# Layer 2's centring pass: eight lines of half the channels a turn, 16 stores instead of 32, half of the last ones issued by ScalarE

## The chip, the cores and the metric

The kernel runs on one core of a Trainium2 chip. Its engines are TensorE (PE, matrix products), VectorE (DVE), ScalarE (ACT) and GpSimd (POOL); SyncE (SP) computes nothing and issues DMAs. Data moves between HBM and the core's memory (SBUF) through 16 DMA engines. The metric is the device time of one execution, in microseconds: 11168.38 us before the change, the median of three runs (11148.58 to 11170.93).

## The reference, cut to what matters

The input is x, 16 images of 64 x 64 positions with 256 channels, float32. Four layers are applied, each as `x = x + layer(groupnorm(x))` with 32 groups. Layer 0 is linear attention with a layer norm, layer 1 a gated block with a scan and two channel reductions, layers 2 and 3 are involutions: at each position a small matrix product makes the weights of a 3 x 3 (layer 2) or 7 x 7 (layer 3) window, one set for each of 16 groups of channels. Layer 3, the one that reads what this change writes, is

```
r    = relu(batchnorm(x @ w_reduce))
kgen = (r @ w_span + b_span).reshape(B, H, W, 16, 49)
xp   = pad(x, 3 rows and columns of zeros on every side)
out  = einsum('bhwgk,bhwkgc->bhwgc', kgen, 7x7 patches of xp)
```

with x here the group-normed input `(x - m) / sqrt(var)`. The subtraction of the mean m must precede the zero padding, since the pad is zero after the norm; the division by the deviation can be moved into the masks and weights.

## The kernel before, in words

The kernel goes through the layers in stages. Layer 0 takes up to about 3600 us of the profiled span, layer 1's scan to about 4190, then comes the stage that ends layer 1 and does layer 2 (to about 7947), then layer 3. Intermediate images lie in HBM: `x2_d` is layer 1's result, `x3_d` layer 2's result as positions by channels, `c3_d` the same as channels by positions, and `strips` the centred and padded copy that layer 3 reads. `strips` holds, for each image and each half of the channels, 73 rows by 14 columns by 8 column tiles by 128 channels: each tile of eight columns is stored with its three neighbours on either side, so that neighbouring tiles overlap.

The stage of layer 2 is a loop of 161 turns (L1154) whose order is written by hand. A turn works on four jobs, each for one eighth of an image, staggered by `LAG = (0, 12, 20, 33)` turns:

- the end of layer 1 (`end_of_layer1`, L897), turns 0 to 127: VectorE, ScalarE, GpSimd, and statistics on VectorE;
- the projection (`projected`, L948), turns 12 to 139;
- the involution, turns 20 to 147: TensorE makes the reduced tile (`reduced2`, L969, from the tile x2r) and the weights (L986) and transposes patches (L1002); VectorE multiplies (`products`, L1040) and sums (L1052, L1053); part of the sums is done by TensorE (L1057);
- the centring (`centred`, L1109), turns 33 to 160: GpSimd subtracts the group mean from a piece of `x3_d` (L1112), and DMAs store it into `strips`.

SyncE issues all DMAs, in the order of the program. In turn n it first issues the loads for the next turns (`loads(n + 1)`, recorded at L872: x2p, x2r, the two x1 pieces and the two pf pieces), then the stores collected in the turn before (L1160: x2_d, x3_d, c3_d and the centring's), then the load of the piece to be centred in the next turn (`load_centred`, tile xc, L890). The profile's names leave numbers out: x2_d and x3_d both read x_d, c3_d reads c_d. The tile xc has two buffers, so that its load in turn n waits until the stores of the buffer's last content, issued just ahead of it in the same turn, have landed. What still lies in the list after the last turn is stored at L1209.

A centring turn takes four lines out of each half of the image (g = 0, 1: lines 0 to 31 and 32 to 63), all 256 channels: 64 columns of each g lie on 128 partitions, a tile of 128 x 4 x 256. A store carries one g, one column tile and one half of the channels: 14 columns (11 at the edges) by 4 lines by 128 channels. That makes 2 x 8 x 2 = 32 stores a turn, in pieces of 512 bytes.

From turn 149 on only the centring is left. Then comes layer 3, whose first loads wait for this stage's memory.

Of the kernel before, what the change touches and what calls it, by code (L numbers as in the profile page):

```python
# [11 lines left out]
ALU = mybir.AluOpType  # L12
# [3 lines left out]
P = 128  # L16
C = 256
HW = 64
NT = HW * HW
NCH = 8  # L20
# [24 lines left out]
def network(ctx: ExitStack, tc: tile.TileContext, a: dict, out: bass.AP):  # L45
    nc = tc.nc
    NI = a["x"].shape[0]
# [44 lines left out]
    strips = dram.tile([NI, 2, HW + 9, TC + 6, NTC, P], F32, tag="strips", name="strips")  # L92
# [10 lines left out]
    def step():  # L103

        for c in list(chains):
            if next(c, c) is c:
                chains.remove(c)
# [47 lines left out]
    with ExitStack() as st:  # L155
# [12 lines left out]
        for v in (wo[:, 0], wo[:, 1], bout):  # L168
            mean = small.tile([P, 1], F32, tag="wmean", name="wmean")
# [17 lines left out]
        loaded, stores = {}, []  # L187

        def load(kind, i, ch):

            if kind == "xin":
                t = []
                for k in range(2):
                    t.append(wk.tile([P, 2, C], F32, tag="xin", name="xin", bufs=4))
                    t0 = ch * CT + k * 256
                    nc.sync.dma_start(
                        out=t[k], in_=a["x"][i, t0 : t0 + 256, :].rearrange("(d p) c -> p d c", p=P)
                    )
            else:
                tag = "xn" if kind == "xn" else "x1"  # L200
                t = wk.tile([P, 2, CT], F32, tag=tag, name=kind, bufs=2 if kind == "xn" else 4)
                src = x_d[i, ch]
                if kind == "xm":
                    src = x1_d[i, :, :, ch * CT : (ch + 1) * CT].rearrange("h p t -> p h t")
                nc.sync.dma_start(out=t, in_=src)
            loaded[kind, i, ch] = t
# [305 lines left out]
        def jobs(n):  # L512
            m, t = divmod(n, NCH)
            i, hf = divmod(m, 2)

            def at(k):
                return 0 <= k < NI

            todo = []
            if at(i):  # L520
                todo.append(("q", i, hf, t))
            if hf == 0:
                if at(i + 1):
                    todo.append(("xin", i + 1, t))
            elif at(i - 1):
                todo.append(("x1", i - 1, t))

            if at(i - 2) and (t >= 2 if hf == 0 else t < 2):
                todo.append(("xm", i - 2, (t - 2) % NCH))
            return todo  # L530
# [4 lines left out]
        def loads(n):  # L535
            for job in jobs(n):
                if job[0] == "q":
                    load("xn", job[1], job[3])
                else:
                    load(*job)  # L540
# [12 lines left out]
        for n in range(2 * NCH * (NI + 1) + NCH + 2):  # L553
            m, t = divmod(n, NCH)
# [54 lines left out]
    with ExitStack() as st:  # L609
# [23 lines left out]
        with tc.tile_pool(name="s_conv", bufs=1) as pcv:  # L633
# [4 lines left out]
                out=lsa.rearrange("p i j c -> p (i j c)"), in_=a["lsa_w"].partition_broadcast(P)  # L638
# [3 lines left out]
            for dj in range(7):  # L642
                dst = band if dj == 0 else term
# [22 lines left out]
        for n in range(10):  # L666
            delta, c = n // 2, n % 2
# [26 lines left out]
        for ch in range(NCH):  # L694
            for b in range(0, NI, 8):
                n = min(8, NI - b)
# [10 lines left out]
                for k, dst in enumerate((pa, pbc[:, 0, :], pbc[:, 1, :])):  # L707
                    nc.tensor.matmul(
                        dst, lhsT=w40[0 : 5 * n, k, :], rhs=rows[0 : 5 * n], start=True, stop=True
# [27 lines left out]
        for k in range(0, NI * NB, P):  # L737
            n = min(P, NI * NB - k)
# [89 lines left out]
    with ExitStack() as st:  # L828
# [7 lines left out]
        gmb = {}  # L836
# [29 lines left out]
        loaded, stores = [], []  # L866
# [8 lines left out]
        def taken(name):  # L875

            n = [k for k, _ in loaded].index(name)
            return loaded.pop(n)[1]
# [9 lines left out]
            ))  # L888

        def load_centred(i, rc):  # L890
            x3n = x3_d[i].rearrange("(g r w) c -> g w r c", g=2, w=HW)
            load("xc", [P, 4, C], *(
                (lambda t, g=g: t[g * HW : (g + 1) * HW], x3n[g][:, rc * 4 : rc * 4 + 4])
                for g in range(2)
            ))

        def end_of_layer1(i, rc):  # L897

            if rc == 0:
                st0[i] = wk.tile([P, 2, NCH, 6], F32, tag="st0", name="st0")  # L900
            x1, pf = taken("x1"), taken("pf")
            zs = [wk.tile([P, 2, 256], F32, tag="z", name="z", bufs=1), pf]
            for h, z in enumerate(zs):
                nc.vector.scalar_tensor_tensor(
                    z, x1[:, h], gm1[:, i, h : h + 1], pf, ALU.subtract, ALU.mult
                )
            yield
            x2 = wk.tile([P, 2, CT], F32, tag="x2", name="x2")
            for h, z in enumerate(zs):
                nc.scalar.activation(  # L910
                    z, z, AF.Relu, bias=bnp[:, 1, h : h + 1], scale=ab[:, 0, i, h : h + 1]
                )
                nc.gpsimd.tensor_tensor(
                    x2[:, h].rearrange("p (t g) -> p g t", g=2), z, x1[:, h], ALU.add
                )
            stores.append((x2_d[i, rc], x2))
            yield
            for h in range(2):
                nc.vector.bn_stats(st0[i][:, h, rc, :], x2[:, h])
            if rc == NCH - 1:  # L920
                chains.append(norm2(i))
                next(chains[-1])
# [185 lines left out]

        def centred(i, rc):  # L1109

            xc = taken("xc")
            nc.gpsimd.tensor_tensor(  # L1112
                xc, xc, gmb[i].unsqueeze(1).broadcast_to([P, 4, C]), ALU.subtract
            )
            for g in range(2):
                r0 = 3 + 32 * g + 4 * rc
                for tj in range(NTC):
                    lo, hi = max(0, tj * TC - 3), min(HW, tj * TC + TC + 3)
                    c0 = lo - tj * TC + 3
                    for h in range(2):  # L1120
                        stores.append((
                            strips[i, h, r0 : r0 + 4, c0 : c0 + hi - lo, tj, :].rearrange(
                                "r w c -> w r c"
                            ),
                            xc[g * HW + lo : g * HW + hi, :, h * P : (h + 1) * P],
                        ))

# [3 lines left out]
        LAG = (0, 12, 20, 33)  # L1133
# [17 lines left out]
        with tc.manual_schedule():  # L1151
            loads(0)
            ahead, made = None, None
            for n in range(TURNS):  # L1154
                end, proj, inv, cen = jobs(n)
                nxt = jobs(n + 1)[2]
                done, stores[:] = list(stores), []
                loads(n + 1)
                for dst, src in done:
                    nc.sync.dma_start(out=dst, in_=src)  # L1160
                nxt_cen = jobs(n + 1)[3]
                if nxt_cen:
                    load_centred(*nxt_cen)
                now, ahead = ahead, None
                ending = end_of_layer1(*end) if end else None
                if ending:
                    next(ending)
                if inv:
                    w1 = weights(now[1], 1)
                    x3 = wk.tile([P, 4, C], F32, tag="x3", name="x3", bufs=3)  # L1170

                def prepare():
                    x2r, rt = reduced2(*nxt)
                    ahead = [x2r, rt]
                    ahead.append(patches(*nxt, lambda: ahead.append(weights(rt, 0))))
                    return ahead

                if nxt and nxt[1]:
                    ahead = prepare()
                if ending:  # L1180
                    next(ending)
                if made:
                    nc.scalar.copy(made[2][:, 0:ON_PE, 0:P], made[3][:, 0:ON_PE])  # L1183
                if inv:
                    los = residual(now[0])
                c3 = turned(*made[:3]) if made else None
                step()
                if proj:
                    projected(*proj)
                if inv:  # L1190
                    pd = products(0, now[2], now[3])
                    sums_on_tensor(pd, los[0])
                if nxt and not nxt[1]:
                    ahead = prepare()
                if inv:
                    pd1 = products(1, w1, now[3])
                    sums(0, pd, los[0], x3)
                step()
                if made:
                    statistics3(*made[:2], c3)  # L1200
                if inv:
                    sums(1, pd1, los[1], x3)
                if ending:
                    next(ending, None)
                made = (*inv, x3, los[0]) if inv else None
                if cen:
                    centred(*cen)
            for dst, src in stores:
                nc.sync.dma_start(out=dst, in_=src)  # L1209
# [309 lines left out]
```

## Time and profile before

The profiled execution spans 11130.4 us. By stage (us; busy times of the engines, share of the DMA engines):

| stretch | length | PE | DVE | ACT | POOL | DMA |
|---|---|---|---|---|---|---|
| 0 to 3600, layer 0 | 3600.00 | 3122.58 | 2236.30 | 1900.12 | 409.75 | 0.41 |
| 3600 to 4190, layer 1's scan | 590.00 | 157.94 | 418.71 | 39.61 | 16.45 | 0.54 |
| 4190 to 7947, end of layer 1 and layer 2 | 3757.00 | 2618.05 | 3259.98 | 1293.71 | 642.96 | 0.53 |
| 7947 to 11130, layer 3 | 3183.40 | 2475.12 | 1610.90 | 1456.49 | 0.00 | 0.56 |

Busy times are sums over the stretch; an engine can be busy beside the others. The profile counts issuing a DMA as no work of an engine, so SyncE has no busy time here; its issues are seen in its timeline, where one line gives start, duration, line, tile and count, and in the chain of waits, where "SPq" is time in which the next step waited for SyncE to issue. The names "out<-in" give a DMA's destination and source.

The DMAs of the centring, with the duration of an issue on SyncE (smallest, median, largest, in ns): 4064 stores into strips at L1160 with 282/387/2124 and 32 at L1209 with 295/387/389; 256 loads of xc with 579/608/988. The subtraction on GpSimd takes 2350 ns (median, 128 times).

### The profile page before, as it was taken

What the parts mean: (1) busy time and instruction counts of PE and PEld (TensorE: products, weight loads), DVE (VectorE), ACT (ScalarE), POOL (GpSimd) and SP (SyncE); (2) the same over time, 40 slices, a digit from 0 to 9 for tenths busy, and PEclk for the clock granted to TensorE, in tenths of its full rate; (3) what the DMA queues carried; (4) which work ended last, traced back from release to release, by engine and by line L of the source; (5) the groups of instructions that cost most, each with busy time, mean ns of one, the idle gap of its engine ahead of it and who ended that gap; (6) DMA issues with size and microseconds to landing.
All of it is one profiled execution on the core that took longest, in us unless ns stands there. A gap on an engine that the chain in (4) does not pass through costs nothing.

```text
span 11130.4 us, 218459 instructions
## 1 busy us (share of the span) xinstructions
PE 8373.7 (75%) x88184; PEld 6128.7 (55%) x88184; DVE 7525.9 (68%) x11694; ACT 4689.9 (42%) x10571; POOL 1069.2 (10%) x681
## 2 busy tenths in 40 slices
PE   8888888888886506777777777774377777777777
PEld 5666666666665204555555555553266655566555
DVE  5566656666665497999999999996155545555444
ACT  4555555555554104343333333332144444444444
POOL 0111111111110002111111111111000000000000
PEclk9999999999998557888888888887699999989999
DMA  7334334433432285455555555544455565555555
GB/s 241 130 133 145 132 127 137 149 127 121 149 107 91 76 289 192 144 175 182 175 174 174 174 174 175 174 142 125 125 172 177 180 204 186 183 180 172 189 186 172
DMA packets 1353717, 1796.61 MB, mean 161 GB/s; under 512 B 132875, under 2 KB 1031812, under 8 KB 1351556
## 3 DMA queue, kind: packets, MB, share of 16 engines
q1 hardware_dynamic: 1352708, 1782.63, 49.8%
q8 instruction: 697, 11.42, 0.4%
q14 instruction: 312, 2.56, 0.1%
HBM read 1268.05 MB, written 536.87 MB: 162 GB/s over the span
## 4 chain that ended last, share of the span: by engine, by line
PE 32%; DVE 18%; DMA 15%; issue 13%; SPq 10%; ACT 9%; POOL 3%; DVEq 0%; ACTq 0%; POOLq 0%
SPq L1160 8%; PE pa L1353 6%; DVE wm L1309 6%; PE pq L267 5%; DMA c_d<-c 5%; PE pk L1294 4%; DMA x<-x_d 4%; PE py L423 4%; PE pr L1262 2%; ACT sq L432 2%; SPq L872 2%; ACT wm L1304 2%; PE px L955 2%; DMA strips<-xc 2%; DVE y L428 1%
## 5 line engine op out<-in xcount | busy, mean ns | idle before, releaser
L267 PE MATMUL pq<-wq,xn 128*128 128x384 f32 x4096 | 1478.0, 500 | 63.1 <-DVE diag L316 21.0
L1040 DVE TENSOR_TENSOR pd<-xs,pw 128x576 f32<-128x576 f32 (+15 forms) x3072 | 1438.0, 549 | 4.5 <-PE pw L986 2.8
L1309 DVE TENSOR_TENSOR wm<-pk,spanb 128x704 f32<-128x704 f32 x896 | 1148.8, 1343 | 216.4 <-PE pk L1294 216.4
L1294 PE MATMUL pk<-rt,span 64*128 64x176 f32 x12288 | 1172.3, 328 | 152.7 <-DVE wm L1309 58.3
L1353 PE MATMUL pa<-wm,xw 126*32 126x48 f32 x45056 | 812.6, 226 | 507.8 <-issue 404.9
L1294 PEld LDWEIGHTS pk<-rt,span 64*128 64x128 f32 x12288 | 934.6, 188 | 385.4 <-ACT wm L1304 183.8
L1304 ACT ACTIVATE wm<-pk,spanb 128x176 f32<-128x176 f32 x2560 | 976.2, 542 | 334.5 <-PE pk L1294 325.9
L1052 DVE TENSOR_REDUCE x<-pd 128x384 f32<-128x3456 f32 (+1 forms) x256 | 1110.9, 4339 | 0.0
L1353 PEld LDWEIGHTS pa<-wm,xw 126*32 126x32 f32 x45056 | 673.4, 123 | 741.8 <-issue 543.6
L1363 DVE SCALAR_TENSOR_TENSOR ex<-pa,msk,ex 128x192 f32<-128x192 f32 x704 | 287.6, 416 | 1171.2 <-ACT ex L1362 1168.8
L267 PEld LDWEIGHTS pq<-wq,xn 128*128 128x128 f32 x4096 | 753.0, 194 | 495.8 <-issue 55.2
L1362 ACT ACTIVATE ex<-pa,msk 128x192 f32<-128x192 f32 x704 | 290.6, 421 | 1034.4 <-PE pa L1353 1031.6
L1006 ACT COPY xs<-pt 128x512 f32<-128x512 f32 x1152 | 606.8, 589 | 117.5 <-PE pt L1002 115.5
L1002 PEld LDWEIGHTS pt<-ident,pad 128*128 128x128 f32 x4608 | 532.4, 149 | 215.3 <-issue 155.6
L1002 PE MATMUL pt<-ident,pad 128*128 128x128 f32 x4608 | 618.2, 289 | 19.1 <-ACT xs L1006 7.7
L976 PE MATMUL pr<-x2r,wrs 128*64 128x512 f32 x512 | 362.9, 849 | 324.0 <-DMA x2r<-x_d 324.0
L979 ACT ACTIVATE rt<-pr,b,sb 64x512 f32<-64x512 f32 x128 | 99.3, 776 | 1134.5 <-PE pr L976 1134.5
L1057 PE MATMUL lo<-pd,ident 128*128 128x128 f32 x2304 | 552.7, 409 | 3.7 <-DVE pd L1040 3.7
L955 PE MATMUL px<-x2p,wis 128*128 128x512 f32 x1024 | 520.8, 653 | 20.5 <-ACT pad L959 10.1
L1057 PEld LDWEIGHTS lo<-pd,ident 128*128 128x128 f32 x2304 | 474.9, 207 | 107.7 <-issue 54.8
L423 PE MATMUL py<-wo,oT 128*128 128x256 f32 x2048 | 484.9, 388 | 61.5 <-DVE va L283 45.3
L1030 PE MATMUL lo<-ident,x2r 128*128 128x128 f32 x896 | 181.7, 330 | 464.0 <-ACT x L1183 294.6
(229 smaller groups left out, 13591.7 us busy)
## 6 DMA issues: line engine op xcount, KB each, us to landing
xw<-strips SPq DMA_DIRECT2D x704, 512.0 KB
xn<-x_d SPq DMA_DIRECT2D x256, 512.0 KB
x<-x_d SPq DMA_DIRECT2D x256, 512.0 KB
x_d<-x SPq DMA_DIRECT2D x256, 512.0 KB
strips<-xc SPq DMA_DIRECT2D x3072, 28.0 KB
xin<-in_x SPq DMA_DIRECT2D x256, 256.0 KB
x_d<-xc SPq DMA_DIRECT2D x128, 512.0 KB
xm<-x_d SPq DMA_DIRECT2D x128, 512.0 KB
```

Of the source, the lines that this page charges most:

```text
L267: nc.tensor.matmul(pq[:, dd, 0:384], lhsT=xn[:, h, tok], rhs=wq[:, h, hf * 384 : (hf + 1) * 384], start=(h == 0), stop=(h == 1),)
L423: nc.tensor.matmul(py[:, q, :], lhsT=oT[hf][:, q * P : (q + 1) * P], rhs=wo[:, hf, :], start=(hf == 0), stop=(hf == 1),)
L955: nc.tensor.matmul(px, lhsT=w[:, h, fh * P : (fh + 1) * P], rhs=x2[:, h], start=(h == 0), stop=(h == 1),)
L1002: nc.tensor.transpose(pt[:, k, h * P : (h + 1) * P], lines[:, h, rc * 4 + e + k, 2 * j : 2 * j + P], ident,)
L1040: nc.vector.tensor_tensor(pd[:, :, o - oh * P : o - oh * P + n, :], xs[dj][:, di : di + 4, c0 : c0 + 9 * n].rearrange("p r (f k) -> p r f ...
L1052: nc.vector.tensor_reduce(half, pd[:, n:], AX.X, ALU.add)
L1057: nc.tensor.matmul(lo[:, 0:ON_PE], lhsT=ident, rhs=pd[:, 0:ON_PE, :, k], start=False, stop=(k == 8))
L1160: nc.sync.dma_start(out=dst, in_=src)
L1294: nc.tensor.matmul(pkv[:, b, m], lhsT=span[half, h * 8 + q * 2 + gg, s0 : s0 + P], rhs=rto[half, o, :], start=True, stop=True,)
L1304: nc.scalar.activation(dst[:, m // 2, m % 2], pkv[:, m // 2, m % 2], AF.Identity, bias=spanb[:, g0 + m : g0 + m + 1],)
L1309: nc.vector.tensor_tensor(dst, pkv, spanb[:, g0 : g0 + 4].rearrange("p (b m) -> p b m", b=2).unsqueeze(3).broadcast_to([P, 2, 2, NTL]), AL ...
L1353: nc.tensor.matmul(pav[32 * q : 32 * q + 32, :, tj * TC : (tj + 1) * TC], lhsT=xws[k][0:TILE_IN, tj, 32 * q : 32 * q + 32], rhs=wm[q][0:TI ...
```

## The change

A centring turn now takes eight lines of one half of the channels instead of four lines of all channels. The turn number rc is split into `q, h = divmod(rc, 2)`: q picks the eight lines, h the half. The tile is 128 x 8 x 128, of the same size, and an image still takes eight turns. A store covers one g and one column tile with 8 lines, so there are 2 x 8 = 16 of them a turn, each of twice the bytes, still in pieces of 512 bytes. The load of xc is still two DMAs; its pieces in HBM are now 512 bytes where they were 1 KB. The second part: in the turns after 148, every other store in the list is issued by ScalarE instead of SyncE. The aim is fewer issues on SyncE, and two issuing engines where only the centring is left.

```diff
         def load_centred(i, rc):
+            q, h = divmod(rc, 2)
             x3n = x3_d[i].rearrange("(g r w) c -> g w r c", g=2, w=HW)
-            load("xc", [P, 4, C], *(
-                (lambda t, g=g: t[g * HW : (g + 1) * HW], x3n[g][:, rc * 4 : rc * 4 + 4])
+            load("xc", [P, 8, P], *(
+                (
+                    lambda t, g=g: t[g * HW : (g + 1) * HW],
+                    x3n[g][:, q * 8 : q * 8 + 8, h * P : (h + 1) * P],
+                )
                 for g in range(2)
             ))
...
+            q, h = divmod(rc, 2)
             xc = taken("xc")
+            mean = gmb[i][:, h * P : (h + 1) * P]
             nc.gpsimd.tensor_tensor(
-                xc, xc, gmb[i].unsqueeze(1).broadcast_to([P, 4, C]), ALU.subtract
+                xc, xc, mean.unsqueeze(1).broadcast_to([P, 8, P]), ALU.subtract
             )
             for g in range(2):
-                r0 = 3 + 32 * g + 4 * rc
+                r0 = 3 + 32 * g + 8 * q
                 for tj in range(NTC):
                     lo, hi = max(0, tj * TC - 3), min(HW, tj * TC + TC + 3)
                     c0 = lo - tj * TC + 3
-                    for h in range(2):
-                        stores.append((
-                            strips[i, h, r0 : r0 + 4, c0 : c0 + hi - lo, tj, :].rearrange(
-                                "r w c -> w r c"
-                            ),
-                            xc[g * HW + lo : g * HW + hi, :, h * P : (h + 1) * P],
-                        ))
+                    stores.append((
+                        strips[i, h, r0 : r0 + 8, c0 : c0 + hi - lo, tj, :].rearrange(
+                            "r w c -> w r c"
+                        ),
+                        xc[g * HW + lo : g * HW + hi],
+                    ))
...
-                for dst, src in done:
-                    nc.sync.dma_start(out=dst, in_=src)
+                for k, (dst, src) in enumerate(done):
+                    tail = n > LAG[2] + NI * NCH and k % 2
+                    (nc.scalar if tail else nc.sync).dma_start(out=dst, in_=src)
```

`LAG[2] + NI * NCH` is 20 + 128 = 148.

## The prediction

> **What bounds the kernel now.** I read the kernel by stage, not by its shares: layer 0 ends near 3600 us, layer 1's scan near 4190, layer 2 near 7947, layer 3 fills the rest. The edit touches only layer 2. There I cut the time at the first instruction of every eighth turn, so that each stretch is one image's eight involution turns, and asked for the busy times. Columns: stretch and length, PE, PEld, DVE, ACT, POOL with counts, clock, DMA share, GB/s.
>
> ```profile
> 4702.30:4907.10 204.80, 157.96 (x815) 118.70 (x816) 199.89 (x293) 81.43 (x163) 40.23 (x26) 0.89 0.57 180
> 5996.20:6221.20 225.00, 166.73 (x815) 121.39 (x815) 204.13 (x298) 80.99 (x163) 41.79 (x27) 0.84 0.56 174
> 7309.80:7508.90 199.10, 156.93 (x799) 112.90 (x800) 181.23 (x255) 69.29 (x146) 19.47 (x9) 0.86 0.48 139
> 7752.80:7946.70 193.90, 0.00 (x0) 0.00 (x0) 0.42 (x1) 0.00 (x0) 25.74 (x11) 0.50 0.32 84
> ```
>
> Read the DVE column against the length. The third image (4702) runs with VectorE 97.6% busy, with centring already in every turn. The ninth (5996) takes 20 us longer for the same work: VectorE is down to 91%. In the last image but one (7309) layer 1's work is gone, VectorE has less to do, and still it idles 9%. In the fourth row no compute engine but GpSimd does anything, and the DMA engines are busy a third of the time. What holds the later images and the end?
>
> The chain of the third image leads through VectorE's products. In the later images and at the end it leads through SyncE (SPq). In the order of the lines: third image, tenth (6221), image 7309, and the end.
>
> ```profile
> by line: DVE pd L1040 18.4%; DVE x L1052 14.8%; SPq L1160 9.8%; DMA c_d<-c 7.9%; DMA x<-x_d 7.2%; PE px L955 5.0%; issue 4.9%; PE lo L1057 4.1%; DMA pf<-fac_d 3.1%; DVE st L919 3.1%; DVE st L1087 2.3%; PE pt L1067 2.1%; DVE z L904 1.9%; DVE
> by line: DMA x<-x_d 18.8%; SPq L1160 17.7%; DMA c_d<-c 9.9%; PE px L955 7.6%; DMA strips<-xc 5.7%; PE lo L1057 5.6%; SPq L872 5.1%; issue 5.0%; ACT xs L1006 3.8%; PE pt L1002 3.4%; PE pr L976 3.4%; DMA x2r<-x_d 3.3%; PE pt L1067 1.9%; PE pw
> by line: SPq L1160 36.8%; DMA c_d<-c 24.2%; PE px L955 7.6%; DMA strips<-xc 6.1%; SPq L872 5.4%; issue 4.7%; DVE x L1052 4.3%; PE lo L1057 4.2%; PE pt L1067 2.0%; PE lo L1030 1.5%; PE pr L976 0.9%; DVE x L1053 0.9%; DVE st L1087 0.6%; ACT x
> by line: SPq L1160 54.8%; DMA xc<-x_d 17.9%; DMA strips<-xc 9.3%; issue 8.5%; SPq L1209 6.0%; SPq L872 4.2%
> ```
>
> SyncE's own timeline shows one of those turns, and then a turn of the end (start, duration, line, what, count):
>
> ```profile
> 6018.78 1.27 SPq L872 DMA_DIRECT2D xc<-x_d  x2
> 6020.09 0.61 SPq L872 DMA_DIRECT2D x2p<-x_d  x1
> 6020.74 0.43 SPq L872 DMA_DIRECT2D x2r<-x_d  x1
> 6021.28 0.93 SPq L872 DMA_DIRECT2D x<-x_d  x2
> 6022.26 2.07 SPq L872 DMA_DIRECT2D pf<-fac_d  x2
> 6024.37 2.33 SPq L1160 DMA_DIRECT2D x_d<-x  x3
> 6027.64 1.43 SPq L1160 DMA_DIRECT2D c_d<-c  x2
> 6029.17 16.76 SPq L1160 DMA_DIRECT2D strips<-xc  x32
> 6047.20 1.27 SPq L872 DMA_DIRECT2D xc<-x_d  x2
> ...
> 7754.15 13.70 SPq L1160 DMA_DIRECT2D strips<-xc  x32
> 7769.20 1.24 SPq L872 DMA_DIRECT2D xc<-x_d  x2
> ```
>
> From one xc load to the next is 28.4 us with hardly a hole: 16.8 us are the 32 stores, then 1.3 us until the stores have landed (the xc load refills their buffer). SyncE's issuing takes the whole turn, so **SyncE is the bound** of the later images; it falls behind slowly, which is why the third image doesn't show it yet. How its lateness reaches VectorE, in the waits of the tenth image (total, times, longest):
>
> ```profile
> PE pr L976 <- DMA x2r<-x_d: 23.8, 6, 6.4
> DVE x L1053 <- PE lo L1057: 13.1, 5, 4.3
> ```
>
> The x2r load is issued late, TensorE starts the next turn's weights late, reaches its sums (L1057) late, and VectorE waits for them. In the third image the first of these waits is absent. The end is plainer: twelve turns of 16.4 us, of which 13.7 are 32 issues, 0.43 us each, with everything else idle.
>
> **What the Trainium skill says.** "DMA: Bandwidth & Descriptors", section "Issuing engines are not separate DMA queues": a second issuing engine saves only issue time, "usually small relative to the DMA itself". The trace disagrees on small: at the end issuing is 13.7 of 16.4 us with the DMA engines at 0.32. Same page, "Rules for kernel authors": under 64 KB a transfer is mostly overhead. The stores are 22 and 28 KB and become twice that; the trace agrees. Same page, "Specifications": below 512 B a piece loses the line rate. The new xc load's pieces are exactly 512 B; the trace's packet records give 27 ns (median) for 512 B against 46 ns for 1 KB, so no cliff, but a piece costs a little more per byte.
>
> **The change part by part.**
>
> *Issue time of a store.* The new store has 8 rows of 512 B on 14 or 11 partitions where the old has 4. No issue of that shape is in the trace, but issue time does not go with bytes: stores on 14 partitions have a median of 387 ns; a load of 64 partitions of 1 KB x 4 (xc) 608 ns, yet one of 64 partitions with 4 bytes each (the constants v) 595 ns, and 128 partitions x 3 pieces of 512 B (ot) 371 ns. So I take 0.43 us a store with its gap; the bound from above is 0.65 (the dearest kind, 0.608 plus gap). Sixteen then take 6.9 us (10.4 at worst) instead of 13.7.
>
> *DMA engines.* Bytes and store packets stay. The load has 1024 packets of 27 ns instead of 512 of 46: 27.6 against 23.6 engine-us, over 16 engines +0.25 us a turn, at a share of 0.56: hidden.
>
> *GpSimd.* Still 1024 elements a partition, one instruction, 2.35 us as now; it waits for xc loads and is busy under 20%: nothing.
>
> *The wait before the xc load* stays: SyncE still waits for the stores just issued, and behind it in the queue stand the next turn's x2p, x2r, x1 and pf loads, on which TensorE and VectorE depend. Stores issued twice as fast land later after the last issue. Lower bound 1.4 us (now); upper 7 us, the time that the c_d stores take to land in the chain of this stage. I take 3. SyncE's turn becomes 27.4 (2191 us over the 80 turns below) - 6.9 + 1.6 = about 22 us, under VectorE's 25.4 (203 us of an image over 8). **The bound goes back to VectorE.**
>
> *Main loop.* The ten images from 5118.8 to 7309.8 take 2191.0 us and have 2023.8 us of VectorE work. At the 97.5% of the third image they take 2076: **-115 us**. Image 7309: 181.2 / 0.965 = 188 instead of 199: **-11**. Earlier images: nothing.
>
> *End.* In turns after 148 half of the stores go to ScalarE, which has no work there, so what queues behind its waits costs nothing. A turn is then 1.3 (xc load) + 8 x 0.43 = 3.4 (both engines at once) + landing. ScalarE's issue price is nowhere in the trace; between 0.4 and 0.65 us, 3.4 to 5.2. Landing: the busiest DMA engines take 16 stores x 8 packets plus 64 of the load, 192 x 29 ns (mean) = 5.6 us, part of it under the issue. So 6.1 us at least (landing 1.4), 11.7 at most (landing 7); I take 7.5. GpSimd is not in the way: xc landed 3.4 us after its issue, plus 2.35, is ready after a turn of this length. Twelve turns: 90 us; the last stores (now 13.4 us, all from SyncE still) 6.9 + 1.4 landing. Together 99 against 209.8 (7736.9 to 7946.7): **-111 us**. Turn 148 itself: **-7**.
>
> Sum: -115 - 11 - 111 - 7 = -244; 11168 - 244 = **10924, rounded to 10925 us**.
>
> **The rivals.**
>
> *Only the end gains.* If the late x2r load comes from the DMA queues (the chain has 10 to 24% on c_d landing) and not from SyncE's issue, the images keep their length: -118, **11050 us**. For it: c_d takes 6 to 7 us to land, and SyncE pauses inside its stores (16.8 instead of 13.7 us). Against it: in the third image the DMA share was as high (0.57) and VectorE did not wait.
>
> *More than that.* VectorE without holes and an end turn of 6.1 us: images -167 and -18, end -128, -7: -320, **10850 us**. For it: nothing else is near its limit. Against: even the image before all centring (4295 to 4494) had VectorE at 96%.
>
> *A wait replaces it, slower.* If the doubled stores, with 512 B loads in front of them, land 10 us after the last issue, SyncE's turn is 1.7 us longer (-6.9 + 8.6), over 95 turns +160; an end turn is 1.3 + 3.4 + 10 = 14.7, -20, and -13 for the single-engine stores: +127, **11295 us**. Against: the DMA engines need 5.6 us for a turn's data even alone.
>
> **How the numbers follow.** Forecast 0.68, only the end 0.12, more 0.14, slower 0.06. The range goes to both neighbours, since landing time (1.4 to 7 us) and ScalarE's price move the sum by some 50 us each way: 10850 to 11055. Faster by over 0.2%: 0.92; same 0.02 (for partial forms of the last rival); slower 0.06.
>
> **What would show it.** Right: 16 issues of 0.39 us a turn; TensorE's wait for x2r nearly gone; images of 205 to 211 us from the fifth on, VectorE at 97%; an end of about 100 us with both engines issuing. Wrong: issue time that grows with the rows; SyncE standing longer before the xc load, with x2r still late; end turns over 10 us. Layers 0, 1 and 3 should not move; if they do, my reading of what the edit touches was wrong.

## The result, and the profile after

The changed kernel takes **10912.13 us** (median of four runs, 10903.33 to 10919.3) against 11162.76 of the kernel before on the same chip (four runs, 11148.58 to 11170.93): a ratio of **0.9776**, 95% interval 0.9759 to 0.9793, or 250.6 us less. 10925 had been predicted.

In the profiled executions, the 3651.1 us from the first involution turn to layer 3's first load (4295.6 to 7946.7) became 3406.3 (4301.1 to 7707.4), 244.8 us less. Ahead of that the two profiles differ by 5.5 us. Layer 3 took 3183.7 us before and 3210.1 after, so the whole spans differ by 212.9 us only (11130.4 and 10917.5). The edit isn't the cause: in the profiles of the eleven kernels below layer 3 lies anywhere from about 3185 to 3211 whether or not they have the edit, and at 3185.5 when the changed kernel was profiled again. What moves it is not known. The single profiles are therefore compared stage by stage, and the whole by the medians.

Stretches of the changed kernel cut at the same turns as in the prediction (length, PE, PEld, DVE, ACT, POOL, clock, DMA share, GB/s). They are the ninth image, the last but one, and the end from turn 149 to layer 3. The last line sums the ten images from the fifth on.

```profile
5950.40:6154.70 204.30, 161.07 (x815) 121.31 (x816) 200.01 (x294) 81.08 (x162) 40.12 (x26) 0.87 0.62 189
7182.60:7361.80 179.20, 151.58 (x799) 114.80 (x800) 175.16 (x250) 68.67 (x147) 19.54 (x9) 0.91 0.55 158
7581.40:7707.40 126.00, 1.19 (x2) 0.50 (x2) 0.97 (x4) 0.00 (x0) 28.72 (x13) 0.50 0.55 138
...
sum 2061.60, PE 1623.75 PEld 1218.25 DVE 2008.52 ACT 805.82 POOL 393.66; mean PE 162.37 PEld 121.83 DVE 200.85 ACT 80.58 POOL 39.37
```

The third image has its 204.8 us as before. The ninth, 225.0 us before, is as short as the third again, with VectorE 97.9% busy, and so it goes on: from the fifth image to the thirteenth the lengths repeat as 208.3, 204.3 and 208.6 us, and the fourteenth, in which layer 1's work runs out, takes 198.0. Layer 2 no longer falls behind. The DMA share has gone up only because the same traffic passes in less time.

SyncE's timeline of one turn of the ninth image (start, duration, line, what, count):

```profile
6014.07 1.29 SPq L872 DMA_DIRECT2D xc<-x_d  x2
6020.77 0.35 SPq L872 DMA_DIRECT2D x2p<-x_d  x1
...
6026.11 2.02 SPq L1168 DMA_DIRECT2D c_d<-c  x2
6031.02 8.25 SPq L1168 DMA_DIRECT2D strips<-xc  x16
6040.92 1.29 SPq L872 DMA_DIRECT2D xc<-x_d  x2
```

Sixteen stores take 8.25 us with their pauses, where 32 took 16.76, and holes have opened: 5.4 us ahead of the x2p load and 2.9 us ahead of the strips stores. What stands in the holes is in SyncE's waits. From 5100 to 7300 us the longest are, first in the kernel before and then in the changed one (total, times, longest):

```profile
SPq L872 <- DMA strips<-xc: 89.8, 151, 2.5
SPq L1160 <- DMA x_d<-x: 89.6, 196, 1.0
SPq L1160 <- DMA c_d<-c: 62.5, 158, 1.2
SPq L1160 <- DMA x2r<-x_d: 55.7, 79, 1.4
```

```profile
SPq L872 <- PE px L959: 503.4, 86, 10.5
SPq L872 <- DMA strips<-xc: 132.2, 194, 2.8
```

Before, stores at L1160 waited in part for the landing of loads whose data they don't use, such as x2r; the reason is found below, with the end turn. SyncE now waits for TensorE (px is its projection, which reads x2p) to finish with the x2p buffer, some 5.9 us in each of the 85 turns of that stretch: it runs ahead of the engines that compute. And TensorE? Over the whole stage from 4200 us the first two of these lines were among its waits before, the third is after (lo are its partial sums). No wait for x2r appears any more. Its waits for ScalarE's copy ahead of the same sums are left out here, since both kernels have them alike (294.6 and 309.8 us).

```profile
PE pr L976 <- DMA x2r<-x_d: 324.0, 76, 8.0
...
PE lo L1030 <- DVE x L1053: 169.0, 33, 10.5
```

```profile
PE lo L1034 <- DVE x L1057: 314.6, 93, 10.5
```

TensorE waited for data; now it waits for VectorE to give buffers back. This is how a bound that moved looks: the same engine idles, for another reason. VectorE's own wait for TensorE's sums fell over the stage from 161.0 us to 56.0:

```profile
DVE x L1053 <- PE lo L1057: 161.0, 66, 6.3
```

```profile
DVE x L1057 <- PE lo L1061: 56.0, 24, 4.2
```

The chain of waits alone would not have told. The third image has the same length and the same share of VectorE in both kernels; its chain led through VectorE's products before, and in the changed kernel it reads

```profile
by line: PE px L959 13.4%; SPq L1168 10.7%; DMA c_d<-c 8.9%; DMA strips<-xc 8.5%; DVE pd L1044 8.0%; SPq L872 7.2%; DVE x L1056 6.5%; issue 5.8%; DMA pf<-fac_d 4.9%; PE pt L1071 4.8%; PE lo L1034 3.4%; DVE st L923 3.1%; POOL xc L1119 2.3%; 
```

So a chain's largest piece is a hint, and the share of VectorE and the runs with less of its work, below, decide.

The end is shorter but not as short as it was predicted. Its timeline in the changed kernel, all engines, in order of start:

```profile
7609.25 20.92 ACTq L1168 DMA_DIRECT2D strips<-xc  x18
...
7614.14 2.34 POOL L1119 TENSOR_TENSOR xc<-xc,gmb 128x1024 f32<-128x1024 f32 x1 [7.85 <-DMA strips<-xc]
...
7619.66 1.26 SPq L872 DMA_DIRECT2D xc<-x_d  x2
7621.02 4.59 SPq L1168 DMA_DIRECT2D strips<-xc  x8
...
7630.01 1.26 SPq L872 DMA_DIRECT2D xc<-x_d  x2
```

From load to load it is 10.3 us, and SyncE's issues, pauses between them included, lie within 5.9 of them. For the rest of the turn SyncE issues nothing. Three questions follow: which part of the change brought what; is it the number of issues, or the new shape of tile and load; and what holds the end turn at 10.3 us.

### The profile page after: what moved, and what is told of

Its sections match the earlier page's. It is cut to its first block, busy times and chain, and to the rows that moved or that the text cites. A ratio compares the mean times of both kernels' runs of the same rounds, so it can differ in the third digit from the quotient of the medians.

```text
span 10917.5 us, 216428 instructions
## 1 busy us (share of the span) xinstructions
PE 8385.3 (77%) x88184; PEld 6195.0 (57%) x88184; DVE 7501.8 (69%) x11694; ACT 4688.3 (43%) x10571; POOL 1066.3 (10%) x681
## 4 chain that ended last, share of the span: by engine, by line
PE 36%; DVE 22%; issue 15%; DMA 10%; ACT 9%; SPq 4%; POOL 4%; ACTq 0%; POOLq 0%; DVEq 0%
PE pa L1361 6%; DVE wm L1317 6%; PE pq L267 5%; PE pk L1302 4%; PE py L423 4%; PE px L959 3%; DVE pd L1044 3%; DVE x L1056 3%; PE pr L1270 2%; SPq L1168 2%; ACT sq L432 2%; DMA c_d<-c 2%; DMA strips<-xc 2%; ACT wm L1312 2%; DMA x_d<-x 2%
## 5 line engine op out<-in xcount | busy, mean ns | idle before, releaser
L1034 PE MATMUL lo<-ident,x2r 128*128 128x128 f32 x896 | 207.4, 365 | 625.1 <-DVE x L1057 314.6
L1006 PEld LDWEIGHTS pt<-ident,pad 128*128 128x128 f32 x4608 | 504.1, 144 | 188.7 <-issue 93.8
L959 PE MATMUL px<-x2p,wis 128*128 128x512 f32 x1024 | 562.9, 697 | 18.1 <-ACT pad L963 10.1
L1061 PE MATMUL lo<-pd,ident 128*128 128x128 f32 x2304 | 553.4, 409 | 16.5 <-DVE pd L1044 16.4
L1034 PEld LDWEIGHTS lo<-ident,x2r 128*128 128x128 f32 x896 | 129.3, 180 | 674.1 <-ACT x L1191 334.6
L423 PEld LDWEIGHTS py<-wo,oT 128*128 128x128 f32 x2048 | 379.0, 191 | 135.3 <-PE po L386 48.9
```

The lines of the kernel that those rows point to most:

```text
L423: nc.tensor.matmul(py[:, q, :], lhsT=oT[hf][:, q * P : (q + 1) * P], rhs=wo[:, hf, :], start=(hf == 0), stop=(hf == 1),)
L959: nc.tensor.matmul(px, lhsT=w[:, h, fh * P : (fh + 1) * P], rhs=x2[:, h], start=(h == 0), stop=(h == 1),)
L1006: nc.tensor.transpose(pt[:, k, h * P : (h + 1) * P], lines[:, h, rc * 4 + e + k, 2 * j : 2 * j + P], ident,)
L1061: nc.tensor.matmul(lo[:, 0:ON_PE], lhsT=ident, rhs=pd[:, 0:ON_PE, :, k], start=False, stop=(k == 8))
```

## The experiments

Each ratio is to the kernel before, measured on the same chip as the experiment (medians there: 11150.64, 11170.04 and 11140.83 us).

**The two parts by themselves.** First the new tile alone: the changed kernel with all stores on SyncE.

```diff
-                for k, (dst, src) in enumerate(done):
-                    tail = n > LAG[2] + NI * NCH and k % 2
-                    (nc.scalar if tail else nc.sync).dma_start(out=dst, in_=src)
+                for dst, src in done:
+                    nc.sync.dma_start(out=dst, in_=src)
```

> The new tile alone: 16 stores of eight lines a turn, all issued by SyncE to the end. My theory: in the changed kernel the two engines do not issue an end turn's stores at the same time; a loop holds the turn (load of xc 4.7 us until the subtraction starts, subtraction 2.34 us, ScalarE's first stores and their landing 3 us, then the next load: 10.3 us). SyncE alone needs 1.3 + 16 x 0.43 + 1.4 to 3 us of landing = 9.6 to 11.2 us a turn, so the end stays at 120 to 140 us and the time equals the changed kernel's within 0.2% (ratio to before 0.976 to 0.980). Rival: the two engines do share the work and the 10.3 us are slow landing; then 8 more issues on SyncE add 3.4 us a turn, 41 us in all, ratio 0.981 to 0.983. The images are as in the changed kernel, 204 to 209 us, in both.

Measured: 10895.4 us, ratio **0.9765** (0.9748 to 0.9782). The images have the lengths of the changed kernel. Its end:

```profile
7609.93 1.26 SPq L872 DMA_DIRECT2D xc<-x_d  x2
7611.23 7.05 SPq L1167 DMA_DIRECT2D strips<-xc  x16
...
7620.11 1.26 SPq L872 DMA_DIRECT2D xc<-x_d  x2
```

10.2 us a turn with one issuing engine, as with two. Next the other part alone, the kernel before with its 32 stores split over the two engines after turn 148:

```diff
-                for dst, src in done:
-                    nc.sync.dma_start(out=dst, in_=src)
+                for k, (dst, src) in enumerate(done):
+                    tail = n > LAG[2] + NI * NCH and k % 2
+                    (nc.scalar if tail else nc.sync).dma_start(out=dst, in_=src)
```

> The old tile and 32 stores a turn, with every other store of the turns after 148 issued by ScalarE: the second part of the change alone. Both theories: the images stay as before (215 to 225 us), since nothing changes before turn 149. My theory (a loop through load, subtraction and ScalarE's stores): ScalarE's 16 stores follow the subtraction, and the next load waits for one of them; an end turn of 11 to 14 us instead of 16.4, -30 to -65 us, ratio 0.994 to 0.997. Rival (the engines share the issues freely): 1.3 + 16 x 0.43 + 1.4 = 9.6 us a turn, -82 us, ratio 0.9925.

Measured: 11107.67 us, ratio **0.9955** (0.9939 to 0.9971). The images take 208 to 225 us as before, and TensorE waits for x2r 335.0 us. The end turns fall from 16.4 to 11.9 us, though each engine issues only 16 of the 32.

So ScalarE is worth something, about 43 us, where SyncE has 32 stores a turn, and nothing on top of the new tile: 0.9765 without it, 0.9776 with it. "DMA: Bandwidth & Descriptors" in the Trainium skill (section "Issuing engines are not separate DMA queues") says that a second issuing engine saves only issue time. These two runs agree, and show that even this is saved only where nothing else stands in its way.

**The number of issues, or the shape?** The tile, the load and the subtraction of the new kernel, all stores on SyncE, but each store cut into two of four lines (32 a turn):

```diff
-                    stores.append((
-                        strips[i, h, r0 : r0 + 8, c0 : c0 + hi - lo, tj, :].rearrange(
...
+                    m = 4
+                    for r in range(0, 8, m):
+                        stores.append((
+                            strips[i, h, r0 + r : r0 + r + m, c0 : c0 + hi - lo, tj, :].rearrange(
+                                "r w c -> w r c"
+                            ),
+                            xc[g * HW + lo : g * HW + hi, r : r + m],
+                        ))
```

The second run has `m = 4 if g else 8`: only the stores of the lower half of the image are cut (24 a turn).

> The new tile, load and buffer, but each store cut into two of four lines, so that SyncE issues 32 a turn again (ScalarE none). Same bytes, same pieces of 512 bytes, same loads as in the changed kernel. My theory (the number of issues on SyncE is what the main loop gains from): the images go back to 215 to 222 us and the end to turns of 16 us, ratio 0.998 to 1.003. Rival (the gain comes from the shape of the tile, contiguous source rows or fewer 1 KB loads): the images keep 204 to 209 us, ratio 0.985 to 0.989 with the longer end.

> Between the new tile alone (16 stores a turn, image 207 us) and the split one (32 stores, image 220 us): only the stores of the lower half of the image (g = 1) are cut in two, 24 issues a turn, all by SyncE. My theory (SyncE's issue time is the bound only when it exceeds VectorE's 25.4 us a turn): SyncE needs about 20.5 to 22 + 8 x 0.43 = 24 to 25.4 us, so the images stay at 206 to 212 us, far less than half of the way to 220; the end is linear in the issues, 13 us a turn, +35 to +40 us; ratio to before 0.979 to 0.984. Rival (every issue delays the loads behind it by its own length, so the loss is linear): images of 213 to 214 us, ratio 0.986 to 0.990.

Measured with 32 stores: 11146.91 us, ratio **0.9994** (0.9984 to 1.0004): the whole gain is gone. The images take 214 to 224 us again, TensorE waits for x2r again (line below), and the end turn is back at 16.4 us, of which 32 issues take 13.6.

```profile
PE pr L980 <- DMA x2r<-x_d: 330.8, 71, 8.1
```

With 24 stores: 10955.01 us, ratio **0.9807** (0.9793 to 0.9822). Its images are those of 16 stores; the tenth:

```profile
6152.50:6361.10 208.60, 162.94 (x815) 122.03 (x816) 203.47 (x302) 81.25 (x162) 40.16 (x26) 0.86 0.60 186
```

208.6 us, the figure of the changed kernel to the tenth, and no wait for x2r. Its end turns take 13.0 us, 2.7 more than those of the changed kernel; twelve of them are 32 of the 36 us by which it gained less (215.0 instead of 250.6). In the loop, then, the number of issues acts as a **threshold**: eight fewer than 32 are as good as sixteen fewer. SyncE's wait for the x2p buffer shows the distance to it: 503.4 us in 85 turns with 16 stores, 206.3 with 24. The eight stores used up 3.5 of 5.9 us a turn; eight more don't fit into the 2.4 that are left. In the end the number acts in proportion.

Cutting a store in two also makes one landing more to wait for. What the runs count is therefore a store in SyncE's queue, with its issue and the pauses that it brings, and not the issue alone.

**Who sets the length of an image?** If SyncE did before and VectorE does now, work taken from VectorE must shorten the images of the changed kernel, and must not shorten those of the kernel before. Both are run with VectorE's statistics in this stage taken over 64 of 512 columns; the rest of them is left out, so the results differ:

```diff
-                nc.vector.bn_stats(st0[i][:, h, rc, :], x2[:, h])
+                nc.vector.bn_stats(st0[i][:, h, rc, :], x2[:, h, 0:64])
...
-                nc.vector.bn_stats(st3[i][:, oh, rc, :], c3[:, oh].rearrange("p g t -> p (g t)"))
+                nc.vector.bn_stats(st3[i][:, oh, rc, :], c3[:, oh, 0, 0:64])
```

> The changed kernel with less work for VectorE: the statistics of the group norms in this stage (L923 and L1091 of it, four instructions a turn) are taken over 64 of 512 columns, so that part of the computation is left out and the result is another. Each falls from 0.68 to about 0.2 us, 1.9 us a turn. My theory (after the change VectorE is the bound of the images): the images fall by 10 to 16 us each, to 191 to 197 us, the whole by 150 to 240 us against the changed kernel. Rival (something else, SyncE's order or TensorE, holds the images at 204 to 209 us): no more than 4 us an image.

> The same removal of VectorE work (statistics over 64 of 512 columns; part of the computation is left out) in the kernel before. My theory (there SyncE's issuing is the bound): only the first two or three images, before SyncE has fallen behind, gain up to 15 us each; from the fifth on they stay at 214 to 225 us. In all -20 to -60 us. Rival (VectorE's own time adds to the turn in both kernels): every image falls by 10 to 16 us, -150 to -240 us.

Measured on the changed kernel: 10725.76 us, ratio **0.9600** (0.9586 to 0.9615), and images of 194 to 195 us, some 13 shorter. Measured on the kernel before: 11151.68 us, ratio **0.9983** (0.9973 to 0.9994), 18.4 us less. Its first three images, in which SyncE has not yet fallen behind, are shorter (184.3, 197.5 and 199.3 us); the fourth to the fourteenth stay at 211 to 226. First an image of the changed kernel with less statistics, then one of the kernel before with less:

```profile
6047.40:6241.50 194.10, 159.24 (x815) 118.65 (x816) 186.87 (x298) 80.85 (x163) 40.16 (x26) 0.89 0.66 198
```

```profile
6195.40:6420.50 225.10, 160.33 (x816) 115.25 (x816) 187.76 (x299) 80.16 (x163) 40.30 (x26) 0.86 0.56 171
```

VectorE does about the same 187 us of work in 194 us here and in 225 there. What it saved in the kernel before went into its own waits: over the stage it stood 258.5 us for TensorE's sums instead of 161.0, and 106.9 for the pf loads, which SyncE issues too, instead of 18.1. TensorE's wait for x2r grew with them, from 324.0 to 381.8 us. The first rival of the prediction, that only the end gains, had failed with the lengths of the images; the run with 32 stores also speaks against its reason, a late landing of the data, since its bytes and pieces are those of the changed kernel.

**What holds the end turn.** The chain of work that ended last in the changed kernel's end, in order of time (start, duration, what), over one turn:

```profile
7616.51 0.31 ACTq L1168
...
7617.30 1.92 DMA strips<-xc
...
7619.24 1.75 DMA strips<-xc
...
7621.02 0.51 SPq L1168
...
7621.58 2.75 DMA strips<-xc
7624.34 2.33 POOL xc L1119
```

ScalarE begins its eight stores of a tile as soon as GpSimd has subtracted (7616.5). SyncE's eight of the same tile begin at 7621.0, after its next xc load, and that load goes out only at 7619.7, when some of ScalarE's new stores have landed. That was not foreseen: the load needs a buffer whose last stores are older. The reason stands in the trace's event records. A completion semaphore is a counter that a DMA raises when its data has landed. Every DMA of this stage, whichever engine issues it, carries one of eight, numbered 101 to 108 and used equally often (844 or 845 times each in the whole kernel), and an issue waits until the last DMA with the same number has landed: for all 3701 DMAs of the stage the number had risen by the full 12, 15 or 16 of its DMA before it was used again. The load at 7619.7 carries 103, and SyncE stands 2.64 us ahead of it, on 108 and 103 (count, then shortest, median and longest in ns):

```profile
L872 SPq EVENT_SEMAPHORE  x3: 28/28/2642, 7616.8 to 7617.0; - x3
```

The last rise of 108 is at 7617.0, and all stores of the load's buffer have landed by then. 103 was carried last by ScalarE's fourth store of the tile just subtracted (issued at 7617.8); its last rise is at 7619.6, where SyncE's wait ends. Ahead of the load at 7630.0 the events show the same with number 105, and 3.60 us. In this loop a turn is 4.7 us from load to subtraction, 2.3 of subtraction, and about 3 of ScalarE's first stores with their landing: 10.3 us.

If an early load, or a buffer free earlier, opens the loop, the turn must get shorter. The first experiment gives xc two buffers more in the end (those of x2p, which are free there); the second also issues the load ahead of the stores; the third does the same with all stores on SyncE. The first line is in all three, the others in the second and third:

```diff
-            ))
+            ), tag="x2p" if i * NCH + rc + LAG[3] > 148 and rc % 2 else None)
...
+                early = n > LAG[2] + NI * NCH
+                if nxt_cen and early:
+                    load_centred(*nxt_cen)
```

> The changed kernel, but in the end turns the loads of xc go by turns into xc's two buffers and into the two buffers of x2p, which are free by then: four buffers, so that a load no longer waits for the stores issued just ahead of it. My theory (a loop of load, subtraction, ScalarE's stores and the buffer's or the completion semaphore's wait sets the 10.3 us): an end turn falls to 6 to 7.5 us, -35 to -50 us against the changed kernel, ratio to before 0.973 to 0.975. Rival (the transfers themselves are that slow when issued twice as fast): the end turn stays over 9 us, ratio 0.977 as the changed kernel.

> The changed kernel with four buffers for xc in the end turns (x2p's two are lent), and there the next xc load issued ahead of the stores instead of behind them; both engines issue stores. If the end turn of 8.1 us with four buffers alone is still a loop through the load's late place in SyncE's queue, it falls to 6 to 7 us, -15 to -25 us against four buffers alone, ratio 0.973 to 0.975. If the completion semaphores, eight for all transfers, or the transfers themselves hold it, it stays at 7.5 to 8.5 us, ratio 0.975 to 0.977.

> Four buffers for xc in the end turns and the load ahead of the stores, as in the run before, but all stores issued by SyncE. If ScalarE's half of the stores is worth nothing in any form, an end turn is SyncE's own issue time, 1.3 + 16 x 0.44 = 8.3 us, and the time equals that of the runs with four buffers and two engines within 0.15% (ratio to before 0.974 to 0.976). If two issuing engines do help once the buffers are free, this one is slower by 3 us a turn or more, ratio 0.977 or above.

Measured: four buffers, 10881.21 us, ratio 0.9754 (0.9737 to 0.9771), turns of 8.1 us on average; load ahead, 10890.28 us, **0.9744** (0.9729 to 0.9758), again about 8.1; load ahead with SyncE alone, 10864.99 us, **0.9752** (0.9738 to 0.9765), turns of 8.4. The chain by line in the end of the last one:

```profile
by line: SPq L1171 71.3%; SPq L872 13.1%; issue 9.9%; DMA xc<-x_d 6.6%
```

There SyncE issues without a hole, 1.3 us of load and 7.0 of stores, and hardly anything else is on the chain. The same view of the kernel with the early load and both engines:

```profile
by line: DMA strips<-xc 51.6%; POOL xc L1119 27.3%; ACTq L1172 10.7%; DMA xc<-x_d 7.0%; SPq L1172 2.4%; issue 2.4%; SPq L872 1.0%; POOLq L1119 0.2%
```

Issuing is down to 14% of the chain, landings and the subtraction make up most of it, and the turn is only 0.3 us shorter. The expectation of 6 to 7.5 us for four buffers was a miss. The last attempt leaves the stores to SyncE with two buffers, as in the tile-only kernel, and gives the loads to ScalarE, so that the wait for landing blocks no store:

```diff
-                nc.sync.dma_start(out=dst(t), in_=src)
+                by.dma_start(out=dst(t), in_=src)
...
+            ), by=nc.scalar if i * NCH + rc + LAG[3] > 149 else nc.sync)
```

> ScalarE issues the loads of xc in the end turns, SyncE all stores; two buffers as in the changed kernel. If the loads' place behind the wait for the landed stores is what costs the end turn (1.3 us of issue plus 1.8 us of waiting), SyncE only has its 16 issues, 7 to 7.5 us a turn, -33 to -40 us against the new tile alone: ratio 0.973 to 0.974. If the two buffers force load, subtraction and stores into a row again (landing 1.8, load 4.7, subtraction 2.3, issue 7), a turn stays at 9 to 11 us: ratio 0.976 to 0.978.

Measured: 10871.42 us, ratio 0.9757 (0.9744 to 0.9771), turns of 9.1 us: 1.1 less than the tile-only kernel, not the whole 1.8 us of waiting and the load's issue. The changed kernel itself ran beside it:

> The changed kernel itself, on the same chip as the two beside it, so that these can be compared with it within a few tenths of a per cent: ratio 0.976 to 0.979, an end of about 126 us with turns of 10.2 to 10.4 us.

Measured: 10887.84 us, ratio 0.9774 (0.9761 to 0.9788), like the first time. On this chip the load ahead with SyncE alone is 22.9 us faster than the changed kernel; twelve turns of 1.9 us less are 23. It is the fastest of those measured beside the change, and the profile accounts for its gain of 0.2%, which is at the edge of what the intervals separate; the ratios of the four kernels with a shorter end can't be told from each other.

## Why the prediction was right

The forecast case came, and its mechanism: SyncE's queue was the bound, and VectorE is now. That the sum came so close is luck, since two errors cancelled. By its steps, predicted and then measured between the marks of the two profiles (us):

| step | predicted | measured |
|---|---|---|
| images 1 to 4 | 0 | -3.3 |
| ten images, 5 to 14 | -115 | -129.4 |
| image 15 | -11 | -19.9 |
| image 16 and the turns to 148 | -7 | -8.4 |
| the end | -111 | -83.8 |
| sum | -244 | -244.8 |

- **Issue time does not grow with rows**: right. The strips stores of 8 rows take 393 ns on SyncE (median, 14 partitions), those of 4 rows took 387. ScalarE's take 331 (median), at most 0.58 us: its price was no risk.
- **SyncE's turn falls to about 22 us, under VectorE's**: right. A turn now takes 25.9 us, of which SyncE waits 5.9 for TensorE, so its own part is about 20. The run with 24 stores shows that the slack was real. One reading of the prediction was too simple: that SyncE's issuing took the whole turn. Summed over the ten images, the issues were 20.3 us of the 27.4 of a turn (44.7 DMAs), the short gaps behind them 1.9, and the other 5 were longer pauses, mostly for landings, as in the wait lines above. Now it is 14.0 us of issues (28.7 DMAs): the fall by 7 us, with gaps, is what was forecast, and the pauses beside the wait for x2p stayed about what they were (4.6 us).
- **The wait before the xc load**: 132.2 us in 85 turns, 1.6 us each, against 3 taken and 7 as a bound. The rival of the slower kernel needed 10.
- **VectorE at 97.5% of the images**: the share was right (2008.5 of 2061.6 us is 97.4%). The work was taken too large: 2023.8 us read in the kernel before, where some VectorE instructions ran longer for the same work. VectorE's instructions in the tenth image show one, before and after:

```profile
L931 DVE TENSOR_SCALAR wis<-wi,gn_r 128x256 f32<-128x256 f32 x2 | 2.8, 1414 | 0.0
```

```profile
L935 DVE TENSOR_SCALAR wis<-wi,gn_r 128x256 f32<-128x256 f32 x2 | 0.7, 349 | 0.0
```

One of the two took 2.48 us before and 0.35 after. Such stretches, in five small instructions of the norms, come to 16 us over the ten images, the 15 us by which the work was taken too large; the term itself fell short by 14. In image 15 (175.16 us of work, not 181.2) two of them are 2.5 of the 6 us; the changed kernel also has five VectorE instructions fewer in that stretch (250 and 255). Why an instruction stretches, no run isolates.
- **The end turn of 7.5 us**: wrong, 10.3. The step that failed is "3.4 (both engines at once)". The two engines don't issue a tile's halves at once, since SyncE's half waits behind its xc load, and that load waits for ScalarE's stores by way of the shared semaphores. Twelve turns of 2.8 us more are 34 us, a little more than the 27 by which the end fell short. The prediction's sentence that what queues behind ScalarE's waits costs nothing looked at ScalarE's queue alone, and not at who waits for ScalarE. That the tile by itself makes the end as short was not seen: ScalarE's half, which the sum took to save some 3.5 us a turn (3.4 instead of 6.9), brought nothing.

Still open is what holds the end at 8.1 us with four buffers and both engines. The DMA share is 0.65 to 0.66 there, so the mean DMA engine isn't full, and the chain runs through landings. The event records point to the eight semaphores. With the early load and both engines, 37 of the 161 issues from 7587.4 to 7659.7 us come after a hole of over 0.07 us and within 0.06 us of the last rise of their own number; with SyncE alone (7574.7 to 7650.8) it is 2 of 161. No run gives the kernel more of them, so this is not shown. That the order of the semaphores also costs the kernel with ScalarE's loads its last microsecond is argued and not shown.

## What to carry to other kernels

Count the DMA issues of a turn, multiply by the time of one, and add the pauses between them: an engine that only issues can be the bound while the profile gives it no busy time, and here the bound showed as a load that came late at another engine. Below the threshold more savings brought nothing, so a cut in issues is worth the distance to the next engine's time and no more. Before a second issuing engine is added, look for what its queue and the first one's share, here buffers and completion semaphores, and try the cheaper half of the change alone.

## What the runs showed of the hardware that was not expected

- Issue time followed neither bytes nor rows on SyncE: a strips store of 14 partitions takes a median of 393 ns with 8 rows and 387 with 4, and an xc load on 64 partitions 618 ns with pieces of 512 bytes and 608 with 1 KB.
- DMAs issued by two engines waited for each other without sharing data. With eight completion semaphores for both queues, SyncE stood 2.64 us for a store of ScalarE's, and eight issues a turn on each engine took as long (10.3 us) as sixteen on one (10.2 us).
- VectorE's busy time is not a fixed amount of work: over ten images with all but the same instructions (2951 and 2956 of them) it was 2023.8 us in the kernel that stalled and 2008.5 in the one that did not.
